# A Macaron block on one core: last attention pair two key blocks at a time, packed reciprocals, moved norm groups and half-width stores

## The chip, the cores and the metric

The kernel runs on one core of one Trainium2 chip. The metric is the device time of one execution in microseconds. Lower is better. The kernel before was run three times for this metric, and once more with the hardware profiler, whose page and trace are what the prediction is made from.

## The reference

The input x has 2048 tokens of 512 floats. The block is

```
x = x + 0.5 * ffn(layernorm(x))
x = x + attention(layernorm(x))
x = x + 0.5 * ffn(layernorm(x))
```

- `ffn` has a hidden size of 4096: `gelu(x @ Wg.T) * (x @ Wu.T)`, then `@ Wd.T`. The three weights come as 4-bit codes with one scale for every 32 values, and both calls use the same weights.
- `attention` is causal, with 16 heads of width 32: `softmax(q k.T / sqrt(32) + mask) v`, a projection in (with bias) and a projection out (with bias).
- `layernorm` subtracts the mean and divides by `sqrt(var + 1e-5)`, with no scale and shift.

All arithmetic is in f32.

## The kernel before

**Three stages.** FFN1 runs from 0 to about 1200 us, attention from about 1200 to 2135, FFN2 from 2135 to the end. x stays in on-chip memory throughout as 16 token tiles `xs` of 128 x 512. A matmul accumulates into a PSUM bank of 128 x 512 f32; the kernel has seven for short-lived results (`ps_one`) and one for the accumulator of attention (`ps_acc`). All instructions stand in the order in which Python emits them, and each engine works through its own queue in that order. DMAs are issued from SP's queue.

**FFN.** The hidden size is cut into 8 groups g of 512. `slot` (L292) computes gate and up for half a group and half the tokens by one level of Strassen: seven products in place of eight, for gate and again for up, so 14 pieces a slot. Sums of token blocks (`token_sums`, L261), of weights and of the results feed it. `down_pieces` (L358) does the product with Wd, also by seven pieces for each of two token pairs q, and adds the results into x. In FFN1 the weights are decoded on VectorE, and are kept in device memory for FFN2. The norms of token blocks 2 and 3 are not done before the FFN starts: `paced` (L138) splits them into groups, and the second slot of group 0 runs one group after each piece (L350). A norm is statistics on VectorE (L98), a square root on ScalarE (L107), a scaling on ScalarE (`xn`, L117) or VectorE, and four transposes on TensorE for each tile (`transpose`, L123). The same function places the norms for attention into the last pieces of FFN1 (L525 to L532). ScalarE also computes GELU (L307), so square root and GELU change its function table. `token_sums` of the second half runs on GpSimd in FFN1 and on VectorE in FFN2 (L482). In `down_pieces` additions that take two on-chip operands run on GpSimd (`add`, L396), and after the last piece of a q in the last group four tiles of x are stored (`finish`, L423).

**Attention.** Heads are taken in eight pairs p. The queries and keys of two pairs share a buffer of 128 partitions (`qT`, `kT`): pair p has rows 0 to 63 when p is even, 64 to 127 when it is odd, 32 rows to a head (`quadrant`, L623). A score matmul contracts over 32 rows, so it uses one quarter of the array's rows. The maxima of each query row must be known before its exponentials: `maxima(p)` (L635) computes scores once with queries on partitions, reduces them on VectorE (L669), splits the maximum into three bf16 parts (L678, GpSimd), and transposes them into `mrow` (L686). `attend(p)` (L699) then computes the scores again with keys on partitions. For a row block g of 512 queries and a block c of 128 keys it emits `maxrows` (a bf16 matmul of the three parts, L746) and `matmuls` (L755) into one bank for each head, and `rest`: on diagonal blocks a copy and a mask (L771, GpSimd's affine_select), then the exponentials on ScalarE (L778). `values` (L706) multiplies with v two blocks later (`pending`). The step loop (L870) runs `attend(p)` and `maxima(p + 1)` side by side, a block of each at a time, so that all four quadrants are in use; the last pair has nothing beside it.

**Denominators.** vaug has 32 columns of ones beside each head's values, so the accumulator holds each head's denominators in 32 identical rows. When row block g is done, ScalarE copies the accumulator into `both` (L720), two DMAs move the denominator rows to the partitions of the values (L725), and four chunks follow, one a step, from the third step on: a reciprocal of 128 x 128 on VectorE (L728) and two multiplies on GpSimd into `attnT` (L731). `divisions` (L736) is a list with one entry a step; it holds a division back on diagonal steps that also carry masks (L806).

**Fills.** Projections are put between diagonal steps: those of q, k and v for later pairs, and `project_out` (L611), whose pieces add `attnT @ wo` into x. In the last pair the pieces of o2 and o3 (of attnT 2 and 3) are spread over the four row blocks and, for g = 3, between steps (L858 to L861). The norms of token blocks 0 and 1 for FFN2 are placed there too (L862 to L868). The last four pieces (`o3[12:]`, L895) need the last chunks of pair 7.

Of the kernel before, what the change touches and what calls it, by code (L numbers as in the profile page):

```python
# [34 lines left out]
def macaron_kernel(ctx: ExitStack, tc: tile.TileContext, x, packed, scales, wqk, bqk, wv, bv, wo, bo, out):  # L35
# [26 lines left out]
    def load_x(tb):  # L62
# [12 lines left out]
    ones_b = const.tile([P, P], BF16, tag="ones_b", name="ones_b")  # L75
    nc.gpsimd.memset(ones_b, 1.0)
    identb = const.tile([P, P], BF16, tag="identb", name="identb")
    make_identity(nc, identb)

    mask_f = const.tile([P, P], F32, tag="mask_f", name="mask_f")  # L80
    nc.gpsimd.memset(mask_f, 0.0)
    nc.gpsimd.affine_select(
        out=mask_f, in_=mask_f, compare_op=ALU.is_ge, fill=MASKED, base=0, pattern=[[-1, P]], channel_multiplier=1
    )
    mask_b = const.tile([P, P], BF16, tag="mask_b", name="mask_b")
    nc.gpsimd.tensor_copy(mask_b, mask_f)
# [51 lines left out]
    def paced(first, second):  # L138

        a, b = [s[:2] + [s[2], s[3], s[5], s[7]] + [s[4], s[6], s[8], s[9]] for s in (first, second)]  # L140
        (a0, a1, *a), (b0, b1, *b) = a, b
        an, at, bn, bt = a[:4], a[4:], b[:4], b[4:]
        return [
            [a0], [a1], [b0, an[0]], [b1, an[1], at[0]], [an[2], at[1]], [an[3], at[2]],
            [bn[0], at[3]], [bn[1], bt[0]], [bn[2], bt[1]], [bn[3], bt[2]], [bt[3]],
        ]
# [7 lines left out]
    def ffn(phase, finish, behind, loads, ready=(), first_w=None):  # L154
# [8 lines left out]
        with tc.tile_pool(name=f"w{phase}", bufs=1) as wp, tc.tile_pool(name=f"dq{phase}", bufs=1) as dq, tc.tile_pool(  # L163
# [97 lines left out]
            def token_sums(tp, eng):  # L261
# [96 lines left out]
            def down_pieces(g, tp, wd, inter):  # L358
# [22 lines left out]
                def piece(i, q):  # L381
# [13 lines left out]

                    def add(dst, other):  # L396
                        nc.gpsimd.tensor_tensor(dst, dst, other, ALU.add)  # L397
# [7 lines left out]
                    elif i == 2:  # L405
                        from_bank(x11, x11)
                        add(x11, u[2, q])
                    elif i == 4:
# [7 lines left out]
                    elif i == 7:  # L416
                        from_bank(u[2, q], u[2, q])
                        add(x21, u[2, q])
                        add(x22, u[2, q])
                    else:  # L420
                        from_bank(u[4, q], u[4, q])
                        add(x12, u[4, q])
                        if g == NG - 1:  # L423
                            for t0 in (8 * tp + 2 * q, 8 * tp + 4 + 2 * q):
                                for t in (t0, t0 + 1):
                                    finish(t)
# [21 lines left out]
            def normed(nm):  # L448
                return ap.tile([P, D], F32, tag="u3", name=nm, bufs=2)
# [8 lines left out]
            if phase == 1:  # L458
# [14 lines left out]
                run(token_sums(0, nc.vector))  # L473
# [5 lines left out]
            else:  # L479
                run(token_sums(0, nc.vector))  # L480
            last_norms = paced(norms[2], norms[3])
            sums = token_sums(1, nc.gpsimd if phase == 1 else nc.vector)  # L482
            last_norms[-1].append(sums[0])
            last_norms += [[s] for s in sums[1:]]
# [49 lines left out]
    def attention(xT, xT_f, wqk_wv, next_w):  # L534
        with tc.tile_pool(name="aw", bufs=1) as aw, tc.tile_pool(name="qk", bufs=1) as qkp, tc.tile_pool(
# [7 lines left out]
            mrow = wo_bo[:, 5 * D :].bitcast(BF16)  # L543
            bqk_sb = aw.tile([P, 2, NQ], F32, tag="bqk", name="bqk_sb")
# [82 lines left out]
            later, divisions = [], []  # L627
# [7 lines left out]
            def maxima(p):  # L635
# [5 lines left out]
                for g in range(NB):  # L641
                    parts = an.tile([P, 2, 4, g + 1], F32, tag=f"parts{g}", name=f"parts_{p}_{g}")
                    steps = [(i, kb) for i in range(4) for kb in range(g)] + [(i, g) for i in (3, 2, 1, 0)]
                    for i, kb in steps:
# [28 lines left out]
                        def finish(now):  # L673
# [12 lines left out]
                            def rows(g=g, sp=sp):  # L686
                                h = slice(64 * (p % 2), 64 * (p % 2) + 64)
                                row = ps_one.tile([P, 512], BF16, tag="one", name=f"row_{p}_{g}")
                                for b in range(4):
                                    nc.tensor.transpose(row[h, bass.ts(b, P)], sp[:, b, :], identb)  # L690
# [8 lines left out]
            def attend(p):  # L699

                q, k, m = qT[(p // 2) % 2], kT[(p // 2) % 2], mrow
# [4 lines left out]
                def values(g, c, off, pt):  # L706
# [11 lines left out]
                    if c == 4 * g + 3:  # L718
                        both = an.tile([P, 512], F32, tag="both", name=f"both_{p}_{g}")
                        nc.scalar.copy(both, av)  # L720

                        rc = dens[g % 2]
                        for a in range(2):
                            v0, d0 = (0, HD) if a == 0 else (3 * HD, 2 * HD)
                            nc.sync.dma_start(out=rc[v0 : v0 + HD, :], in_=both[d0 : d0 + HD, :])  # L725

                        def chunk(j):
                            nc.vector.reciprocal(rc[:, bass.ts(j, P)], rc[:, bass.ts(j, P)])  # L728
# [7 lines left out]
                        divisions.extend([None] * 2 + [lambda j=j: chunk(j) for j in range(4)])  # L736

                for g in range(NB):
                    for c in range(4 * g + 4):
                        off = max(0, c - 4 * g) * P  # L740
                        ps = [None, None]

                        def maxrows(a):
                            r = quadrant(p, a)
                            ps[a] = ps_one.tile([P, 512], F32, tag="one", name=f"ps_{p}_{g}_{c}_{a}")
                            nc.tensor.matmul(  # L746
                                ps[a][:, off:],
                                lhsT=ones_b[r.start : r.start + 3, :],
                                rhs=m[r.start : r.start + 3, g * 512 + off : (g + 1) * 512],
                                start=True, stop=False,  # L750
                            )

                        def matmuls(a):
                            r = quadrant(p, a)
                            nc.tensor.matmul(  # L755
                                ps[a][:, off:],
                                lhsT=k[r, bass.ts(c, P)],
                                rhs=q[r, g * 512 + off : (g + 1) * 512],
                                start=False, stop=True,
                            )  # L760

                        def rest():
                            pt = pp.tile([P, 2, 512], F32, tag="pt", name=f"pt_{p}_{g}_{c}")
                            scale = 1.0 / math.sqrt(HD)
                            plain = off
                            if c >= 4 * g:

                                plain = off + P
                                own = pt[:, :, off:plain]
                                for a in range(2):  # L770
                                    nc.scalar.copy(own[:, a], ps[a][:, off:plain])  # L771
                                nc.gpsimd.affine_select(
                                    out=own, in_=own, compare_op=ALU.is_ge, fill=MASKED, base=0,
                                    pattern=[[0, 2], [1, P]], channel_multiplier=-1,
                                )
                            if plain < 512:
                                for a in range(2):
                                    nc.scalar.activation(pt[:, a, plain:], ps[a][:, plain:], AF.Exp, scale=scale)  # L778
                            if plain > off:
                                nc.scalar.activation(own, own, AF.Exp, scale=scale)  # L780
                            pending.append(lambda args=(g, c, off, pt): values(*args))
                            if len(pending) > 2:
                                pending.pop(0)()

                        yield maxrows, matmuls, rest, c >= 4 * g
# [14 lines left out]
            def after_step(diagonal, fill, masks):  # L800
# [4 lines left out]

# [182 lines left out]
```

## Time and profile before

| | us |
|---|---|
| median of three runs | 3313.41 |
| lowest, highest | 3310.98, 3314.13 |
| the profiled execution | 3312.17 |
| its span | 3310.4 |
| last pair of attention, with its tail | 2013.45 to 2135.38 |
| TensorE busy in the span | 3265.4 |
| VectorE busy | 2117.7 |
| GpSimd busy | 1153.2 |
| ScalarE busy | 870.3 |

The mean granted clock of TensorE was 0.998. The profiled execution lies 1.8 us above its span and 1.2 us below the median.

Reading it: PE is TensorE's matmul, PEld its weight load, DVE is VectorE, ACT ScalarE, POOL GpSimd, SP the engine that issues DMAs (SPq its queue). A line of the timeline gives the start, the duration, the engine, the line of the code, the operation with output and input, its shapes, and how many were joined into the line; brackets give the idle time before it and what ended it. In a table by windows each engine has its busy time and number of instructions, then come the granted clock (1.00 is full), the share of DMA time and GB/s.

### The profile page before, as it was taken

Reading aid. Unit: us, or ns where it says so; the run is one execution under the profiler, and the core shown is the slowest. Engines: PE = TensorE matmul, PEld = TensorE weight load, DVE = VectorE, ACT = ScalarE, POOL = GpSimd, SP = SyncE. Lnnn points to the kernel's source line nnn. Section 1 sums busy time; section 2 is a strip of 40 time slices with the busy share of each in tenths; the row PEclk is TensorE's granted clock in tenths of the full one; section 3 lists DMA queues with packets and bytes.
Section 4 is the critical chain, followed back from the end, with each engine's and each line's share of the span. In section 5 each row is a group of like instructions: output and inputs, shape, how many; then the busy total and the mean of one; then the engine's idle time right before and its main releaser. Section 6 shows DMA issues by size and latency. Waiting matters only on the chain.

```text
span 3310.4 us, 34022 instructions
## 1 busy us (share of the span) xinstructions
PE 3265.4 (99%) x12640; PEld 1724.7 (52%) x12640; DVE 2117.7 (64%) x3222; ACT 870.3 (26%) x1798; POOL 1153.2 (35%) x1333
## 2 busy tenths in 40 slices
PE   7999999999999999999999999999999999999998
PEld 3556565655656565333343333346555565655556
DVE  7977777777778556686766784455455455445545
ACT  4111111111111131454444555431111111111111
POOL 2646464554637341332221222103132222313223
PEclk9999999999999999999999999999999999999999
DMA  3111111111111100000000000100011101101101
GB/s 133 61 57 64 64 48 64 70 61 52 63 64 48 67 16 9 4 14 7 12 6 4 30 6 7 48 23 29 38 45 45 45 23 45 36 31 47 43 23 51
DMA packets 37943, 132.75 MB, mean 40 GB/s; under 512 B 3984, under 2 KB 20368, under 8 KB 31376
## 3 DMA queue, kind: packets, MB, share of 16 engines
q1 hardware_dynamic: 37776, 130.57, 10.7%
q8 instruction: 100, 1.64, 0.2%
q14 instruction: 67, 0.55, 0.1%
HBM read 78.12 MB, written 48.23 MB: 38 GB/s over the span
## 4 chain that ended last, share of the span: by engine, by line
PE 95%; DVE 1%; issue 1%; ACT 1%; POOL 1%; DMA 0%; POOLq 0%; SPq 0%; DVEq 0%; ACTq 0%
PE po L386 23%; PE pu L287 23%; PE pg L287 22%; PE av L711 8%; PE pm L654 6%; PE pqk L577 3%; PE ps L746 3%; PE ps L755 2%; PE pp L616 2%; PE pv L594 2%; PE pt_f L127 0%; DVE parts L669 0%; PE pt_a L127 0%; PE row L690 0%; DVE st_f L100 0%
## 5 line engine op out<-in xcount | busy, mean ns | idle before, releaser
L386 PE MATMUL po<-wd,inter 128*128 128x256 f32 x2048 | 482.5, 379 | 0.0
L287 PE MATMUL pg<-xT_f,w 128*128 128x512 f32 x1024 | 477.8, 594 | 0.0
L287 PE MATMUL pu<-xT_f,w 128*128 128x512 f32 x1024 | 476.0, 592 | 0.0
L386 PEld LDWEIGHTS po<-wd,inter 128*128 128x128 f32 x2048 | 388.9, 190 | 155.1 <-issue 104.8
L397 POOL TENSOR_TENSOR x<-x,d 128x512 f32<-128x512 f32 x256 | 340.0, 1340 | 346.1 <-DVE d L394 171.8
L341 POOL TENSOR_TENSOR u<-u,u 128x512 f32<-128x512 f32 x128 | 163.4, 1277 | 836.4 <-ACT u L338 832.1
L669 DVE TENSOR_REDUCE parts<-pm 128x1 f32<-128x512 f32 (+3 forms) x640 | 367.3, 604 | 92.9 <-PE pm L654 81.5
L386 PE MATMUL po<-wd,s 128*128 128x256 f32 x1536 | 362.2, 379 | 0.0
L287 PE MATMUL pg<-xsum,w 128*128 128x512 f32 x768 | 355.6, 592 | 3.2 <-POOL xsum L269 1.3
L287 PE MATMUL pu<-xsum,w 128*128 128x512 f32 x768 | 355.7, 592 | 0.0
L386 PEld LDWEIGHTS po<-wd,s 128*128 128x128 f32 x1536 | 291.6, 190 | 116.3 <-issue 79.6
L654 PE MATMUL pm<-kT,qT 32*128 32x512 f32 (+3 forms) x1280 | 337.7, 574 | 0.5 <-DVE parts L669 0.4
L778 ACT ACTIVATE pt<-ps 128x512 f32<-128x512 f32 (+3 forms) x576 | 271.8, 530 | 149.1 <-PE ps L755 148.1
L711 PE MATMUL av<-pt,vaug 128*64 128x512 f32 (+3 forms) x1280 | 304.1, 554 | 0.8 <-ACT both L720 0.6
L287 PEld LDWEIGHTS pg<-xT_f,w 128*128 128x128 f32 x1024 | 195.3, 191 | 193.4 <-issue 180.1
L287 PEld LDWEIGHTS pu<-xT_f,w 128*128 128x128 f32 x1024 | 194.2, 190 | 190.8 <-issue 181.3
L755 PE MATMUL ps<-qT,kT 32*128 32x512 f32 (+3 forms) x1280 | 292.8, 531 | 0.0
L287 PEld LDWEIGHTS pg<-xsum,w 128*128 128x128 f32 x768 | 145.5, 190 | 148.6 <-issue 136.6
L287 PEld LDWEIGHTS pu<-xsum,w 128*128 128x128 f32 x768 | 145.7, 190 | 143.4 <-issue 136.6
L394 DVE SCALAR_TENSOR_TENSOR x<-po,x 128x512 f32<-128x512 f32 x192 | 131.6, 686 | 115.8 <-ACT d L401 85.6
L731 POOL TENSOR_TENSOR attnT<-both,den 32x128 f32<-32x128 f32 x256 | 115.7, 452 | 242.1 <-DVE den L728 173.3
L394 DVE SCALAR_TENSOR_TENSOR d<-po,d 128x512 f32<-128x512 f32 x192 | 131.8, 686 | 86.2 <-PE po L386 84.2
(129 smaller groups left out, 3650.1 us busy)
## 6 DMA issues: line engine op xcount, KB each, us to landing
kept<-wd SPq DMA_DIRECT2D x8, 1792.0 KB
wd<-kept SPq DMA_DIRECT2D x8, 1792.0 KB
x<-in_x SPq DMA_DIRECT2D x16, 256.0 KB
pk<-in_gate_codes SPq DMA_DIRECT2D x16, 256.0 KB
sc<-in_gate_scales SPq DMA_DIRECT2D x32, 128.0 KB
pk<-in_up_codes SPq DMA_DIRECT2D x16, 256.0 KB
sc<-in_up_scales SPq DMA_DIRECT2D x32, 128.0 KB
pk<-in_down_codes SPq DMA_DIRECT2D x16, 256.0 KB
```

What stands on the lines that cost most here:

```text
L287: nc.tensor.matmul(ps, lhsT=a[:, j, :], rhs=b[:, j, :], start=(j == 0), stop=(j == 1))
L341: nc.gpsimd.tensor_tensor(u4, u4, u2, ALU.add)
L386: nc.tensor.matmul(ps[:, j, :], lhsT=a[i][:, k, bass.ts(2 * q + j, P)], rhs=b[i][:, k, :], start=(k == 0), stop=(k == 1),)
L394: stt(dst, ps, 0.5, other, ALU.mult, ALU.add)
L397: nc.gpsimd.tensor_tensor(dst, dst, other, ALU.add)
L577: nc.tensor.matmul(ps, lhsT=w[:, j, k, :], rhs=xT[tb][:, k, :], start=(k == 0), stop=(k == 3))
L654: nc.tensor.matmul(ps[a][:, :n], lhsT=q[r, bass.ts(4 * g + i, P)], rhs=k[r, kb * 512 : kb * 512 + n], start=True, stop=not on_pe,)
L669: nc.vector.tensor_reduce(parts[:, a, i, kb : kb + 1], ps[a][:, :n], AX.X, ALU.max)
L711: nc.tensor.matmul(av[64 * a : 64 * a + 64, off:], lhsT=vaug[:, c, p % 4, HD * a : HD * a + 2 * HD], rhs=pt[:, a, off:], start=(c == 0), s ...
L731: nc.gpsimd.tensor_tensor(dst[quadrant(p, a), bass.ts(4 * g + j, P)], both[v, bass.ts(j, P)], rc[v, bass.ts(j, P)], ALU.mult,)
L755: nc.tensor.matmul(ps[a][:, off:], lhsT=k[r, bass.ts(c, P)], rhs=q[r, g * 512 + off : (g + 1) * 512], start=False, stop=True,)
L778: nc.scalar.activation(pt[:, a, plain:], ps[a][:, plain:], AF.Exp, scale=scale)
```

## The change

1. **Last pair.** `attend` takes a width. Pair 7 is done with width 2: each step holds two key blocks, and their scores use all four quadrants. For this, at the start of pair 6, two DMAs copy rows 64 to 127 of pair 7's q and k to rows 0 to 63 of the other buffer, and the rows of maxima of pair 7 are transposed into both halves of `mrow`. Twice as many PSUM banks are taken by a step. The pieces of `project_out` that stood in the last diagonal steps stand after the loop, in front of and behind the last divisions.
2. **Reciprocals.** For pairs 0 to 6 one denominator row for each head goes by DMA to device memory (`flat`), comes back as 16 x 64 (`packs`), gets one small reciprocal four steps later, and goes back to device memory and, broadcast, to `den`. The multiplies follow from eight steps after the copy. Pair 7 keeps the direct way. `divisions` is keyed by step and holds nothing back.
3. **Norms and sums.** In `paced` the first normalised tile comes one group later, after both statistics groups of the second block; the list for the second slot starts with an empty group and takes the last three sums of `token_sums` in one group. `token_sums` is always on VectorE. xn has buffers of its own in place of those of u3.
4. **End.** In the last group, for the second half of tokens and q = 1, the additions run on VectorE. x is stored in quarters of a pair of tiles (two tiles, half the columns), each as soon as it is complete.
5. **Constants.** `ones_b`, `identb`, `mask_f` and `mask_b` are made at the start of attention.

```diff
@@ def paced
-            [a0], [a1], [b0, an[0]], [b1, an[1], at[0]], [an[2], at[1]], [an[3], at[2]],
+            [a0], [a1], [b0], [b1, an[0]], [an[1], at[0]], [an[2], at[1]], [an[3], at[2]],
             [bn[0], at[3]], [bn[1], bt[0]], [bn[2], bt[1]], [bn[3], bt[2]], [bt[3]],
@@ ffn
-            def token_sums(tp, eng):
+            def token_sums(tp):
+                eng = nc.vector
...
+                    adder = nc.vector if (g, tp, q) == (NG - 1, 1, 1) else nc.gpsimd
                     def add(dst, other):
-                        nc.gpsimd.tensor_tensor(dst, dst, other, ALU.add)
+                        adder.tensor_tensor(dst, dst, other, ALU.add)
+                    def done(second, half, x_):
+                        if g == NG - 1:
+                            finish(8 * tp + 2 * q + 4 * second, half, x_)
...
-                return ap.tile([P, D], F32, tag="u3", name=nm, bufs=2)
+                return ap.tile([P, D], F32, tag="xn", name=nm, bufs=2)
...
-            sums = token_sums(1, nc.gpsimd if phase == 1 else nc.vector)
+            sums = token_sums(1)
+            last_norms = [[]] + last_norms
             last_norms[-1].append(sums[0])
-            last_norms += [[s] for s in sums[1:]]
+            last_norms.append(sums[1:])
@@ maxima
-                                h = slice(64 * (p % 2), 64 * (p % 2) + 64)
+                                halves = (p % 2,) if p + 1 < NPAIR else (0, 1)
+                                h = slice(64 * halves[0], 64 * halves[-1] + 64)
...
-                                    nc.tensor.transpose(row[h, bass.ts(b, P)], sp[:, b, :], identb)
+                                    for i in halves:
+                                        nc.tensor.transpose(row[64 * i : 64 * i + 64, bass.ts(b, P)], sp[:, b, :], identb)
@@ values
+                        direct = p == NPAIR - 1
...
+                            flat = store.tile([2, 512], F32, tag=f"flat{g % 2}", name=f"flat_{p}_{g}")
+                            packs = an.tile([16, 64], F32, tag="packs", name=f"packs_{p}_{g}")
+                            for a in range(2):
+                                d0 = HD + HD * a
+                                nc.sync.dma_start(out=flat[a : a + 1, :], in_=both[d0 : d0 + 1, :])
+                            nc.sync.dma_start(out=packs, in_=flat.rearrange("a (j n) -> (a j) n", j=8))
+                        def inverse():
+                            nc.vector.reciprocal(packs, packs)
+                            back = store.tile([2, 512], F32, tag=f"back{g % 2}", name=f"back_{p}_{g}")
+                            nc.sync.dma_start(out=back.rearrange("a (j n) -> (a j) n", j=8), in_=packs)
+                            for a in range(2):
+                                v0 = 3 * HD * a
+                                nc.sync.dma_start(out=rc[v0 : v0 + HD, :], in_=back[a].partition_broadcast(HD))
                         def chunk(j):
-                            nc.vector.reciprocal(rc[:, bass.ts(j, P)], rc[:, bass.ts(j, P)])
+                            if direct:
+                                nc.vector.reciprocal(rc[:, bass.ts(j, P)], rc[:, bass.ts(j, P)])
...
-                        divisions.extend([None] * 2 + [lambda j=j: chunk(j) for j in range(4)])
+                        if not direct:
+                            at(4, inverse)
+                        for j in range(4):
+                            at((3 if direct else 8) + j, lambda j=j: chunk(j))
@@ attend
+                    i = 0 if copied else (p // 2) % 2
+                    q, k = qT[i], kT[i]
+                    def rows_of(a):
+                        return slice(HD * a, HD * a + HD) if copied else quadrant(p, a)
...
-                    for c in range(4 * g + 4):
+                    for c in range(0, 4 * g + 4, width):
+                        yield [step(g, c + i, i > 0) for i in range(width)]
@@ the loop over pairs
-                    fills = [o2[:4], o2[4:8], o2[8:12] + o3[:4], o2[12:] + o3[8:12]]
+                    fills = [o2[:4], o2[4:8], o2[8:12] + o3[:4], []]
...
+                if p + 2 == NPAIR:
+                    for t in (qT, kT):
+                        nc.sync.dma_start(out=t[0][0:64, :], in_=t[1][64:128, :])
+                n = 0
+                for steps in attend(p, 2 if p + 1 == NPAIR else 1):
...
                     for a in range(2):
-                        maxrows(a)
+                        for maxrows, _, _, _ in steps:
+                            maxrows(a)
...
                     for a in range(2):
-                        matmuls(a)
+                        for _, matmuls, _, _ in steps:
+                            matmuls(a)
...
-                    rest()
-                    after_step(diagonal, fill, other is not None)
-                    for step in extra.get(n, ()):
-                        step()
+                    for _, _, rest, _ in steps:
+                        rest()
+                    for _, _, _, diagonal in steps:
+                        after_step(diagonal, fill)
+                        for step in extra.get(n, ()):
+                            step()
+                        n += 1
...
-            for step in divisions:
-                if step:
+            rest = o2[12:] + o3[8:12]
+            for piece in rest[:4]:
+                piece()
+            for when in sorted(divisions):
+                for step in divisions[when]:
                     step()
-            for piece in o3[12:]:
+            for piece in rest[4:] + o3[12:]:
                 piece()
@@ the output
+    def store_out(t, half, x_):
+        rows = out[t * P : (t + 2) * P, half * 256 : half * 256 + 256]
+        nc.sync.dma_start(out=rows.rearrange("(j p) n -> p j n", p=P), in_=x_)
```

## The prediction, made before the changed kernel ran

> **What bounds the kernel now.** I read the page's first part, the chain that ended last, then the timeline by stage.
>
> ```profile
> PE 3265.4 (99%) x12640; PEld 1724.7 (52%) x12640; DVE 2117.7 (64%) x3222; ACT 870.3 (26%) x1798; POOL 1153.2 (35%) x1333
> ...
> PE 95%; DVE 1%; issue 1%; ACT 1%; POOL 1%; DMA 0%; POOLq 0%; SPq 0%; DVEq 0%; ACTq 0%
> ```
>
> TensorE is busy 99% of 3310.4 us and is 95% of the chain. Time taken from another engine counts only where TensorE waits for it, and such places sum to some 45 us. So two things can pay: fewer TensorE microseconds, or one of the few idle places.
>
> One block of scores in attention, first in pair 6 (which also computes the maxima of pair 7), then in pair 7 (which has no next pair):
>
> ```profile
> 1999.84 0.38 PE L746 MATMUL ps<-wo_bo,ones_b 3*128 3x512 bf16 x1
> 1999.84 0.69 PE L654 MATMUL pm<-kT,qT 32*128 32x512 f32 x1
> ...
> 2000.06 0.60 PE L755 MATMUL ps<-qT,kT 32*128 32x512 f32 x2
> 2000.37 0.60 PE L654 MATMUL pm<-kT,qT 32*128 32x512 f32 x2
> 2000.49 0.60 PE L755 MATMUL ps<-qT,kT 32*128 32x512 f32 x2
> 2001.02 1.08 PE L711 MATMUL av<-pt,vaug 128*64 128x512 f32 x4
> 2002.03 0.38 PE L746 MATMUL ps<-wo_bo,ones_b 3*128 3x512 bf16 x1
> ```
>
> ```profile
> 2050.80 0.39 PE L746 MATMUL ps<-wo_bo,ones_b 3*128 3x512 bf16 x2
> ...
> 2051.03 1.02 PE L755 MATMUL ps<-qT,kT 32*128 32x512 f32 x4
> ...
> 2051.98 1.08 PE L711 MATMUL av<-pt,vaug 128*64 128x512 f32 x4
> ...
> 2052.99 0.39 PE L746 MATMUL ps<-wo_bo,ones_b 3*128 3x512 bf16 x2
> ```
>
> The reader is to see one thing: 1999.84 to 2002.03 is 2.19 us, and 2050.80 to 2052.99 is 2.19 us as well. Four row quadrants (two of scores, two of maxima) take the 1.18 us that two take. Half the rows of the array stand empty in pair 7.
>
> The end of attention:
>
> ```profile
> 2122.92 0.87 PE L711 MATMUL av<-pt,vaug 128*64 128x256 f32 x8
> 2129.36 6.19 PE L616 MATMUL pp<-wo_bo,attnT 128*128 128x512 f32 x8 [5.56 <-POOL attnT L731]
> 2135.38 1.88 PE L287 MATMUL pg<-xT_f,w 128*128 128x512 f32 x4
> ```
>
> ```profile
> 2013.50:2123.80 110.30, 110.09 (x502) 37.17 (x500) 43.91 (x73) 58.31 (x140) 22.54 (x54) 1.00 0.02 6
> 2123.80:2129.40 5.60, 0.04 (x1) 0.05 (x1) 2.26 (x3) 0.59 (x1) 0.92 (x3) 0.84 0.10 23
> 2129.40:2135.40 6.00, 6.00 (x9) 2.52 (x10) 3.18 (x5) 0.00 (x0) 2.69 (x6) 0.58 0.00 0
> ```
>
> TensorE waits 5.56 us for copy, DMA, reciprocal and multiply, and then runs its last four pieces at a granted clock of 0.58: 6.19 us for what takes 4 x 1.06 = 4.24 elsewhere.
>
> **Last pair by two blocks.** By width 512, 384, 256, 128 the scores of a block took 1.18, 0.91, 0.66, 0.43 us. Before: 24 full blocks and four diagonals, 24 x 1.18 + 4 x 3.18 = 41.0 us. After, with both blocks of a step side by side and the wider one setting the time: 12 x 1.18 + 4 x (1.18 + 0.66) = 21.5. That takes away 19.5 us. The values (1.01 us per full block) stay.
>
> Eight projection pieces (8.5 us) leave the last diagonals and stand between the last values and the four dependent pieces. The last pair becomes 110.3 - 19.5 - 8.5 = 82.3 us, the tail 12 x 1.06 = 12.7 us. The first multiply ends about 5.5 us after the last values and the last one 8.7 us after, so 8.5 us of pieces cover the chain and the clock stays up. Together 95.0 against 121.9 (2013.45 to 2135.38): -26.9 us if nothing waits.
>
> Something will wait. The Trainium skill, "TensorEngine Tiling (Array Packing)", section Performance Considerations, speaks against this edit: packing speeds TensorE but not the emptying of PSUM, which may become the bottleneck. The rows: four exps are 2 x 1.08 = 2.16 us of ScalarE per double step, against 1.18 + 2 x 1.01 = 3.20 us on TensorE, so by the row the steady steps stay TensorE's and the whole 26.9 stand. But a double step holds four of the seven banks where a single one held two, so a ScalarE pause once covered by three steps is now covered by less than one. There is such a pause:
>
> ```profile
> 2083.22 1.28 ACT L107 ACT_TABLE_LOAD   x1
> 2086.47 0.30 ACT L107 ACTIVATE rstd_f<-mv_f,eps 128x4 f32<-128x4 f32 x1 [1.96 <-DVE mv_f L101]
> 2086.78 1.28 ACT L778 ACT_TABLE_LOAD   x1
> ```
>
> The square root of the norms stops the exps from 2083.22 to 2088.08, 4.86 us, without a TensorE wait today. In the new order its statistics stand on VectorE behind a reciprocal of the same row block that waits for its DMA, so I make the pause 6 us and the stall 6 less about 2 of cover: 4.0. The second norm group, placed the same way: 2.8. The first double step of three row blocks, where the copy of the accumulator stands behind four exps: 3 x 0.9. The last diagonals, without pieces between them (VectorE and GpSimd chain mask, exp, values): 1.65. The start: 0.3. Sum 11.5; bounds 0 and 18 (all of this plus a cold clock). By the row -26.9, by the rule's logic **-15.4**, which I take.
>
> Two copies of 512 KB (q and k rows 64 to 127 to rows 0 to 63) go onto SP's queue at the start of pair 6, ahead of the denominators of pair 5; a pair (over 80 us) lies before their first reader: 0, at worst 3 us once. The rows of maxima of pair 7 are transposed for both halves: four times four more transposes; a set took 0.39 us, so up to 1.6, and I take **+1.2**.
>
> **Packed reciprocals** (pairs 0 to 6, 28 places). Removed: 4 x 0.94 us of VectorE each (the reciprocal of den, 128 times, 119.6 us busy), less about 0.2 for the packed one: some 100 us of VectorE. TensorE's waits for VectorE or the accumulator copy in all pairs sum to 1 us, so this is worth about **0**. It adds a chain: copy 0.59, two issues of 0.51, landing 1.93, issue 0.51, landing 1.93, about 6 us, before a reciprocal emitted four steps later; four steps are 8.8 us in the long stretches, and about 5.8 at the shortest. Then back and two broadcasts (5 to 6 us) before multiplies four steps further on. Two of its hops go through device memory and no near row exists; bounds -3 (the three longest steps at the first row block of a pair lose some of their VectorE wait) and +22 (below). If it is late, behind the waiting reciprocal stand the maxima's reductions, with two banks each; behind the waiting multiply stand the mask operations.
>
> **Norm groups later, sums on VectorE.** In each FFN's second slot the second block's square root now comes before the first block's normalisation, so ScalarE's table changes square root, GELU, square root, GELU: two more loads per slot. Row: a load is 1.28 us and the next exp starts 1.30 after it. The skill, "ScalarE: Activation LUTs", What ACT_TABLE_LOAD costs, has 2.66 us per switch with the drain; the trace shows no such drain. By the row the first normalised tile of FFN1 comes at 65.0 instead of 59; by the page some 2.8 us later still, in both slots (forecast 5.6 us up). I take the row. FFN1's slot ran 35.4 us against 27.75 of work (waits 3.27, 0.64, 1.14, then 1.26 for GpSimd's xsum, and a clock of 0.66 after the longest). Later: one wait of 5.7 with the same cold stretch after it, and VectorE's sums (1.22 to 1.36 us against 2.35 to 2.80) remove the last wait: **-0.8**. FFN2's slot ran 33.1 (waits 1.01, 2.06, 1.14, clock 1.00); one wait of 4.85 and cold: **+1.4** (0.7 to 2.1). The norms at FFN1's end (waits 0.59 and 1.46 today): **+1.0** (0 to 2.5). Between FFN1 and attention the statistics come a little later: **+0.6**; the constants moved there (six GpSimd operations) run while GpSimd is free. xn's own buffers: 0 or a small gain.
>
> **The end.**
>
> ```profile
> 3301.16 3.71 POOL L397 TENSOR_TENSOR x<-x,d 128x512 f32<-128x512 f32 x3 [0.81 <-DVE d L394]
> ...
> 3304.90 2.00 SPq L923 DMA_DIRECT2D out<-x  x4
> ```
>
> Four stores follow the last sum, and the span ends at 3310.4. With the last additions on VectorE (0.69 where GpSimd takes 1.25) the last sum is done about 1.1 us sooner, and one store instead of four remains behind it (3 x 0.5): **-2.7** (-1.5 to -3.5).
>
> **Sum.** -15.4 + 1.2 + 0 - 0.8 + 1.4 + 1.0 + 0.6 - 2.7 = -14.7 us. The profiled execution took 3312.2 (span 3310.4 and 1.8 around it), giving 3297.5; the median of the runs is 3313.4, giving **3299**.
>
> **Rivals.**
> - *No stalls in the double steps.* For it: ScalarE is at 58.3 of 110.3 us in the last pair. Against: the 4.86 us pause and four banks a step. -14.7 - 11.5 = -26.2: 3287.
> - *The gain is given back in place.* Stalls of 18 instead of 11.5, and the page's table cost for 2 to 3 us: -14.7 + 6.5 + 2.5: 3308. For it: 0.58 after a wait of 5.56, 0.66 after 3.27. Against: 1.00 after 2.06.
> - *Slower: the packed chain is late.* The reciprocal waits on VectorE in order, the reductions behind it hold the banks of maxima, and TensorE stops at each of 28 places. One step of cover (2.2) is allowed for; it decides from (14.7 + 6.6) / 28 = 0.76 us each, that is from about 5.8 + 2.2 + 0.76 = 8.8 us between the last values and the landing. At 1.0 us each: 3299 + 28 = 3327. Against: my 6 us.
> - *Packing does not pay* when all four quadrants carry maxima rows and scores: only tail and end are left, about 3313 - 7: 3306. The 2.19 in both pairs speaks against it.
>
> **Chances.** Forecast 0.50, no stalls 0.22, given back or not paying 0.22, late chain 0.06. A measurement of this kernel tells about 0.2% (6.6 us) from no change. Faster 0.84 (all but half of the third case and the last), same 0.10, slower 0.06. The range 3285 to 3309 leaves out the late chain, the top of the third case and the bottom of the second.
>
> **What would show it.** Right: pair 7 with double steps of 3.2 us and a stall by the square root near its 15th; no 0.58 stretch before FFN2; four more table loads; one store after the last sum. Wrong: TensorE waiting in pairs 0 to 6 with VectorE's packed reciprocal as releaser, or double steps of 4.4 us.

## The result and the profile after

The changed kernel took 3298.16 us (median of five runs, 3296.2 to 3300.15) against 3312.97 for the kernel before, a ratio of 0.9956 with a 95% interval of 0.9941 to 0.9970: 14.8 us faster. The forecast was 3299. The profiled execution is the slowest of the five (3300.15, span 3298.4), so its span is 12.0 us shorter than that of before. One of the five executions of e1 below, the profiled one, ran at a granted clock of 0.65 and took 4810 us; it is left out, so no trace of e1 is read.

The parts of the page that answer to those shown of before, engines and chain:

```profile
PE 3249.1 (99%) x12656; PEld 1723.4 (52%) x12656; DVE 2043.7 (62%) x3152; ACT 872.9 (26%) x1802; POOL 1128.3 (34%) x1319
...
PE 94%; DVE 3%; ACT 2%; issue 1%; POOL 0%; DMA 0%; SPq 0%; POOLq 0%; DVEq 0%; ACTq 0%
```

TensorE has 16.3 us less work and is as full as before; VectorE has 74 us less, and what that is worth is tried in e2. Where the 12.0 us went is read by cutting both traces at the same instructions:

| stretch | before | after | difference |
|---|---|---|---|
| start to first gate product | 22.8 | 24.0 | +1.2 |
| to the first down product (holds FFN1's second slot) | 89.0 | 88.5 | -0.5 |
| to the first q/k projection (holds the norms at FFN1's end) | 1088.4 | 1090.5 | +2.1 |
| to the first scores of pair 0 | 100.7 | 100.7 | 0.0 |
| pairs 0 to 6 | 711.8 | 710.6 | -1.2 |
| pair 7 and tail, to FFN2's first product | 122.7 | 107.0 | -15.7 |
| to FFN2's first down product (holds its second slot) | 84.2 | 89.7 | +5.5 |
| to FFN2's last product | 1082.2 | 1082.2 | 0.0 |
| to the end of the span | 8.6 | 5.3 | -3.4 |

The start differs by 0.2 to 1.2 us among the executions of kernels that have the same code there; it is not the change. Pairs 0 to 6 took 711.8 us before, in e3 and in e9, and 713.4 in e4 and e10, whose code there is also that of before; with packed reciprocals they took 709.1 in e2, e6 and e7, and 710.4 to 710.8 in the changed kernel, e5, e8 and e11. In every case the longer ones have a stretch of 3.4 us at half clock between 1410 and 1420 us into the span, and the shorter ones do not. So the -1.2 of the table is -2.7 from the reciprocals and +1.5 from that stretch.

Pair 7 in the changed kernel, TensorE's timeline and then ScalarE's, around the first square root:

```profile
2075.00 0.39 PE L790 MATMUL ps<-wo_bo,ones_b 3*128 3x512 bf16 x4
2075.23 1.03 PE L799 MATMUL ps<-qT,kT 32*128 32x512 f32 x8
2076.18 1.94 PE L729 MATMUL av<-pt,vaug 128*64 128x512 f32 x8
...
2079.11 0.39 PE L790 MATMUL ps<-wo_bo,ones_b 3*128 3x512 bf16 x2
2082.12 0.86 PE L790 MATMUL ps<-wo_bo,ones_b 3*128 3x512 bf16 x2 [2.63 <-ACT pt L822]
2082.62 1.38 PE L799 MATMUL ps<-qT,kT 32*128 32x512 f32 x8
```

```profile
2074.36 1.28 ACT L95 ACT_TABLE_LOAD   x1
2079.87 0.30 ACT L95 ACTIVATE rstd_f<-mv_f,eps 128x4 f32<-128x4 f32 x1 [4.22 <-DVE mv_f L89]
2080.18 1.28 ACT L822 ACT_TABLE_LOAD   x1
2081.48 2.07 ACT L822 ACTIVATE pt<-ps 128x512 f32<-128x512 f32 x4
```

Two blocks of scores now take the 1.18 us from 2075.00 to 2076.18 that one took before. Then the exps stop from 2074.36 to 2081.48, 7.1 us, and TensorE, with half its maxima rows of the next step already out, finds no free bank for 2.63 us. That is what the prediction named; what its sum did not hold is in the last line of the first view, where 1.03 has become 1.38: soon after the wait TensorE runs at half clock, 0.50 in the third column from the end.

```profile
2083.58:2086.98 3.40, 3.40 (x12) 0.77 (x8) 0.00 (x0) 2.06 (x4) 0.17 (x1) 0.50 0.00 0
```

A table by windows, pair 7 and its tail (the column before the last two is the granted clock):

```profile
2014.27:2110.73 96.46, 87.43 (x495) 30.94 (x493) 35.66 (x64) 57.26 (x143) 22.69 (x54) 0.95 0.03 6
2110.73:2121.29 10.56, 10.56 (x26) 4.42 (x26) 8.97 (x14) 0.59 (x1) 3.61 (x8) 1.00 0.06 13
```

The clock was 1.00 in this stretch before. It is 0.95 now: three stretches of 3.4 us at half clock. The tail is full and at full clock.

The tail and FFN2's start, TensorE, then VectorE:

```profile
2110.66 10.79 PE L625 MATMUL pp<-wo_bo,attnT 128*128 128x512 f32 x24
2121.29 3.60 PE L276 MATMUL pg<-xT_f,w 128*128 128x512 f32 x8
...
2126.86 5.37 PE L276 MATMUL pg<-xsum,w 128*128 128x512 f32 x8 [1.98 <-issue]
```

```profile
2115.01 3.38 DVE L765 RECIPROCAL den<-den 128x128 f32<-128x128 f32 x4
...
2118.30 4.81 DVE L628 TENSOR_TENSOR x<-pp,x 128x512 f32<-128x512 f32 x8
...
2123.03 1.22 DVE L256 TENSOR_TENSOR xsum<-xT_f 128x1024 f32<-128x1024 f32 x1
```

Twelve pieces take 10.6 us, 0.88 each when they stand in a row. But their additions on VectorE are held up by the reciprocals, eight of them end at 2123.1, and only then come the sums of tokens that FFN2's third product needs. TensorE waits 1.98 us (1.05 before), and those products take 5.37 us for 3.6 at half clock.

The first norm tile of FFN1's second slot, and the end of the kernel (SP's queue and VectorE):

```profile
65.66 1.13 PE L115 MATMUL pt_f<-ident,xn_f 128*128 128x128 f32 x4 [4.95 <-ACT xn_f L105]
```

```profile
3293.24 2.30 SPq L985 DMA_DIRECT2D out<-x  x3
3293.73 0.68 DVE L383 SCALAR_TENSOR_TENSOR d<-po,d 128x512 f32<-128x512 f32 x1
3294.45 0.69 DVE L389 TENSOR_TENSOR x<-x,d 128x512 f32<-128x512 f32 x1
```

One wait has taken the place of three, as forecast. At the end one store, the third of the first line (issued at 3295.17), is left behind the last addition.

### The profile page after: what moved, and what is told of

The parts are those of the page before. It is cut to its first block, busy times and chain, and to the rows that moved or that the text cites. A ratio compares the mean times of both kernels' runs of the same rounds, so it can differ in the third digit from the quotient of the medians.

```text
span 3298.4 us, 34148 instructions
## 1 busy us (share of the span) xinstructions
PE 3249.1 (99%) x12656; PEld 1723.4 (52%) x12656; DVE 2043.7 (62%) x3152; ACT 872.9 (26%) x1802; POOL 1128.3 (34%) x1319
## 4 chain that ended last, share of the span: by engine, by line
PE 94%; DVE 3%; ACT 2%; issue 1%; POOL 0%; DMA 0%; SPq 0%; POOLq 0%; DVEq 0%; ACTq 0%
PE po L375 23%; PE pu L276 23%; PE pg L276 22%; PE av L729 8%; PE pm L668 6%; PE pqk L586 3%; PE ps L790 2%; PE pp L625 2%; PE pv L603 2%; PE ps L799 2%; ACT pt L822 1%; DVE st_f L88 0%; PE pt_f L115 0%; PE pt_a L115 0%; DVE parts L683 0%
## 5 line engine op out<-in xcount | busy, mean ns | idle before, releaser
L389 POOL TENSOR_TENSOR x<-x,d 128x512 f32<-128x512 f32 x248 | 329.7, 1340 | 344.7 <-DVE d L383 170.8
L799 PE MATMUL ps<-qT,kT 32*128 32x512 f32 (+3 forms) x1280 | 277.5, 534 | 0.0
L816 POOL TENSOR_SCALAR_AFFINE_SELECT pt<-pt 128x256 f32<-128x256 f32 x128 | 52.1, 407 | 388.0 <-ACT pt L815 387.8
```

The lines of the kernel that those rows point to most:

```text
L389: adder.tensor_tensor(dst, dst, other, ALU.add)
L799: nc.tensor.matmul(ps[a][:, off:], lhsT=k[r, bass.ts(c, P)], rhs=q[r, g * 512 + off : (g + 1) * 512], start=False, stop=True,)
```

## The experiments

All times are medians; ratios are to the kernel before on the same chip, with 95% intervals. The changed kernel, e1 to e4, e5 to e8 and e9 to e12 each ran beside a kernel before of their own, with medians of 3312.97, 3312.26, 3312.24 and 3312.35. So where a time of e5 to e12 is set against the changed kernel's 3298.16, 0.6 to 0.7 us of the gain is that difference. The intervals reach 2 to 4.5 us to either side; what small steps rest on is the stretches of the traces. My theory was the sum of the prediction: nearly all from the last pair, a little from the end, some lost on the norms. The rivals: the packed reciprocals carry part of the gain; the parts are only worth something together.

**Each part alone.** The kernel before with one part of the change. e1 has the last pair and its tail:

```diff
-                for n, (...) in enumerate(attend(p)):
+                for steps in attend(p, 2 if p + 1 == NPAIR else 1):
...
+            rest = o2[12:] + o3[8:12]
```

> Kernel before with the last-pair part alone (double steps, rows of maxima for both halves, pieces moved behind the loop). My theory, as in the prediction: -15.4 + 1.2 = -14.2 us. From the profile of the changed kernel: from the end of pair 6 to the first FFN2 product it took 107.0 us against 122.7, so -15.7. Rival, the packed reciprocals carry part of the gain: less than 12 us here.

Measured 3295.01, ratio 0.9945 (0.9932 to 0.9959): -17.3 us. The rival (under 12 us) falls. The gain is more than the theory's 14.2, and more than the whole change brought.

e2 has the packed reciprocals (`flat`, `packs`, `inverse`, chunks from the eighth step):

> Kernel before with the packed reciprocals alone (pairs 0 to 6). My theory: 0 us, within 1. Rival, the chain costs: slower by 5 or more. Second rival, VectorE's 100 us do count: faster by 3 or more. In the profile of the changed kernel pairs 0 to 6 are 1.2 us shorter.

Measured 3309.03, ratio 0.9991 (0.9983 to 0.9999): -3.2 us, at the edge of what can be told from nothing and more than my 0. The trace says where. The starts of all 280 steps of pairs 0 to 6 were compared: one step in each of row blocks 1, 2 and 3, the third, where the accumulator of the row block before is copied, went from about 3.0 to 2.8 us, together -3.7 over the seven pairs; a few others gave back 1.0, which leaves the -2.7 of pairs 0 to 6 in this trace. One such step of pair 3 before:

```profile
1663.82 0.94 DVE L728 RECIPROCAL den<-den 128x128 f32<-128x128 f32 x1
...
1664.49 0.59 PE L654 MATMUL pm<-kT,qT 32*128 32x512 f32 x1
...
1664.68 1.22 DVE L669 TENSOR_REDUCE parts<-pm 128x1 f32<-128x512 f32 x2
...
1666.03 0.38 PE L746 MATMUL ps<-wo_bo,ones_b 3*128 3x512 bf16 x1
```

and with packed reciprocals:

```profile
1663.27 1.41 DVE L683 TENSOR_REDUCE parts<-pm 128x1 f32<-128x512 f32 x2 [0.50 <-PE pm L668]
1663.36 0.59 PE L668 MATMUL pm<-kT,qT 32*128 32x512 f32 x1
...
1664.91 0.39 PE L790 MATMUL ps<-wo_bo,ones_b 3*128 3x512 bf16 x1
```

Before, a reciprocal of 0.94 us stands on VectorE between two pairs of reductions. After, VectorE is waiting for TensorE there. The step before ran from 1663.02 to 1666.03, now from 1662.11 to 1664.91. That the reductions gave the banks back late is read from these lines; it was not tried by itself.

e3 has the norm groups, the sums and xn's buffers (with the moved constants, whose room they take):

```diff
-            [a0], [a1], [b0, an[0]], [b1, an[1], at[0]], ...
+            [a0], [a1], [b0], [b1, an[0]], [an[1], at[0]], ...
```

> Kernel before with the moved norm groups, token sums on VectorE, xn's own buffers and the moved constants (these two belong together, since the buffers take the room of the constants). My theory as in the prediction: -0.8 + 1.4 + 1.0 + 0.6 = +2.2 us. From the profile of the changed kernel: -0.5 in FFN1's slot, +2.1 at FFN1's end and up to +5.4 in FFN2, so about +7. Rival, the part gains because the three short waits become one: -3.

Measured 3316.42, ratio 1.0012 (1.0006 to 1.0019): +4.2 us. The part costs time, more than the prediction's +2.2 and less than the +7 read from the changed kernel. Its trace has the wait of 4.29 us in each slot, -0.5 for FFN1's slot, +0.5 at FFN1's end and +2.4 in FFN2's. The -0.5 is not the part's doing: in e2, e4, e9 and e10, whose code there is that of before, the same slot is 0.5 to 0.8 us shorter than in the one trace of before.

e4 has the end (`adder`, `done`, `store_out`):

> Kernel before with the end alone (last additions on VectorE, output stored by halves). My theory: -2.7 us. From the profile of the changed kernel: -3.4. Rival, the smaller stores cost more at the queue: 0 or slower.

Measured 3309.48, ratio 0.9990 (0.9982 to 0.9998): -2.8 us; in its trace the stretch after the last product is 3.5 us shorter.

The four sum to -17.3 - 3.2 + 4.2 - 2.8 = -19.1, against -14.8 for all. The four intervals together are about as wide as that difference, so it is not shown that the parts work against each other. The granted clock is where the difference could lie: it was 0.997 to 0.998 in the four runs of e1 and 0.994 or 0.995 in the five of the changed kernel, and 0.001 of 3300 us is at most 3.3 us of TensorE's time (an estimate; half clock under a wait costs less).

**The last pair in two halves.** e9 has the double steps, with the pieces where they were; e10 only moves the pieces, by this edit:

```diff
-                    fills = [..., o2[12:] + o3[8:12]]
+                    fills = [..., []]
```

> Kernel before with the double steps alone: the pieces of the output projection stay in the last diagonal steps. My theory: scores -19.5 us, stalls and half clock in the last pair +7, transposes +1.2, the tail as before: about -11. Rival, the double steps bring nearly all of the -17.3 that both together measured: -15 or more.

Measured 3300.98, ratio 0.9967 (0.9954 to 0.9979): -11.4 us, as the theory had it; the rival falls. Pair 6, in which 12 of the 16 added transposes stand, took 81.49 us in its trace and in that of before.

> Kernel before with the moved pieces alone: the last pair stays at one block a step. My theory: the wait of 5.56 us and the half clock of about 1.9 go, -7.4, less about 1 where the last diagonal steps lose their cover: -6. Rival, the half clock only moves to FFN2's start (its wait for the sums of tokens): -4.

Measured 3305.24, ratio 0.9979 (0.9973 to 0.9986): -7.1 us. The trace adds what the total hides: the last pair and tail are 8.0 us shorter and FFN2's beginning 2.9 us longer, by the wait already seen in the changed kernel, here with one block a step:

```profile
2128.34 3.60 PE L287 MATMUL pg<-xT_f,w 128*128 128x512 f32 x8
2133.92 5.37 PE L287 MATMUL pg<-xsum,w 128*128 128x512 f32 x8 [1.98 <-issue]
```

So the moved pieces alone make it. The rival had the right place, the theory the better size. In the traces e9 and e10 shorten pair 7 and tail by 11.5 and 8.0 us, and the changed kernel, with both, by 15.7; by the medians they sum to -18.5, against -17.3 in e1. Whether the two gains overlap stays open.

**The norms.** e5 takes the norm part out of the changed kernel (the constants stay moved):

> Changed kernel with the norm groups, the token sums and the xn buffers as before. My theory now: the norm part costs what it cost alone, +4.2, and some 3 us more that only the whole change shows in FFN2, so 3298.2 - 4 to 7 = 3291 to 3294. Rival, the parts are not additive because of the last pair alone: about 3298, no change.

Measured 3293.21, ratio 0.9942 (0.9930 to 0.9955): 4.9 us under the changed kernel (4.2 when each is taken against its own kernel before), which agrees with e3.

e6 swaps two steps in one group, so that the first tile is normalised before the second half of the second block's statistics and its square root:

```diff
-            [a0], [a1], [b0], [b1, an[0]], [an[1], at[0]], ...
+            [a0], [a1], [b0], [an[0], b1], [an[1], at[0]], ...
```

> Changed kernel with two steps of one norm group swapped: the first normalised tile is emitted before the second half of the second block's statistics, so before its square root. My theory, the wait of about 5 us in each second slot comes from this tile standing behind the second square root and the two table loads before it: the wait of 4.95 in FFN1 and 4.29 in FFN2 falls under 3, and the time by 4 to 8 us. Rival, VectorE's statistics are what is late whatever the order on ScalarE: within 1 us of the changed kernel.

Measured 3290.89, ratio 0.9935 (0.9922 to 0.9947): 7.3 us under the changed kernel (6.5 against its own kernel before). FFN1's slot is 2.4 us shorter than the changed kernel's, FFN1's end 3.9, FFN2's slot 1.9. The wait of 4.95 in FFN1's slot became

```profile
62.52 0.74 PE L115 MATMUL pt_f<-ident,xn_f 128*128 128x128 f32 x4 [2.67 <-ACT xn_f L105]
...
66.77 0.74 PE L115 MATMUL pt_f<-ident,xn_f 128*128 128x128 f32 x4 [1.79 <-ACT xn_f L105]
```

4.46 us of waiting in two pieces, and in this execution no half clock at all in FFN1, where the changed kernel had 6.8 us of it in the slot and 3.4 at the end. The swap changes nothing in the order of VectorE's queue, so the order on ScalarE is the cause, and not VectorE's statistics. About half of the gain is the clock: of the 8.2 us in these three stretches 4.0 are waits of TensorE and 4.2 its busy time.

e7 fills the wait with matmuls whose result is not used:

```diff
+            def warm():
+                ps = ps_one.tile([P, 512], F32, tag="one", name=f"warm_{phase}")
+                for _ in range(4):
+                    product(ps, second.factors(0)[1], token_factors(0)[1])
```

> Changed kernel with 8 matmuls of 128x512 more (3.4 us at full clock, result unused) on TensorE in each second slot, just before the first transpose that waits. If the half clock after the wait is a cost of its own (6.8 us at half clock in each slot, so 3.4 us lost), these slots are 2 to 3.4 us shorter each, the time 4 to 7 us. Rival, the clock costs nothing beyond the wait or goes down anyway: 0, or longer by what does not fit into the wait.

Measured 3299.31, ratio 0.9959 (0.9947 to 0.9972): no change, where the theory had 4 to 7 us. The eight matmuls took 7.03 us and not the 3.4 I had put down:

```profile
60.08 7.03 PE L276 MATMUL warm<-xT_f,w 128*128 128x512 f32 x16
```

That still answers the question: 7.03 us of work put in the place of a 4.95 us wait made FFN1's slot 0.25 us shorter. Wait and half clock together had cost 7.03 + 0.25 = 7.3 us, so the half clock about 2.3 of them. That is for this one place. For the changed kernel and then this one, the windows of the wait and of the work after it, and of the filled stretch:

```profile
60.60:65.60 5.00, 0.11 (x1) 0.00 (x0) 4.13 (x12) 3.52 (x5) 0.65 (x1) 0.73 0.11 46
65.60:72.50 6.90, 6.80 (x18) 3.45 (x19) 1.01 (x2) 4.74 (x8) 0.00 (x0) 0.70 0.00 0
```

```profile
50.00:66.00 16.00, 16.00 (x38) 7.03 (x37) 13.27 (x31) 9.08 (x12) 5.03 (x5) 1.00 0.32 132
66.00:84.50 18.50, 18.46 (x67) 10.17 (x66) 6.71 (x10) 11.44 (x19) 1.27 (x1) 1.00 0.00 0
```

**The square roots.** e8 does those of pair 7 on VectorE: an integer shift and subtraction for a first value, and three Newton steps, 12 instructions on 128 x 4 (the expectation counts 13):

```diff
-                nc.scalar.activation(rstd, mv[:, :, 1], AF.Sqrt, bias=eps)
-                nc.vector.reciprocal(rstd, rstd)
+                if not on_act:
+                    inverse_root()
+                else:
+                    ...
```

> Changed kernel with the two square roots of the last attention pair done on VectorE (13 small instructions, by shift, subtraction and three Newton steps) instead of ScalarE, so without the four table loads there. My theory, the pause of ScalarE stops the double steps: the wait of 2.63 us and the half clock after it go, 3 to 5 us faster than the changed kernel. Rival, the pause is covered and the stall has to do with VectorE's order: 0.

Measured 3294.71, ratio 0.9942 (0.9929 to 0.9956): 3.5 us under the changed kernel (2.7 against its own kernel before), at the low end of the theory. In its trace pair 7 and tail are 3.6 us shorter. The wait of 2.63 for a bank is gone, so the pause of ScalarE was its cause; one of 1.25 for VectorE's normalised tile stands there, and 2.75 at the second block. All idle time of TensorE in pair 7 is 8.7 us for 9.0, so most of the gain is in its busy time, with two stretches of half clock there in place of three.

e11 is both, the version to which the experiments point:

> Changed kernel with the swapped norm steps of e6 and the square roots of the last pair on VectorE of e8. If both causes are separate, the gains add: 3298.2 - 7.3 - 3.5 = 3287, against 3312.3 before. Rival, both only bring the clock back once: about 3290.

Measured 3286.88, ratio 0.9924 (0.9912 to 0.9937): 25.5 us faster than before, 11.3 than the changed kernel. That is the sum of the two gains. The rival's 3290 lies within the interval, so the traces decide: against the changed kernel, FFN1's slot is 2.4 us shorter, FFN1's end 3.8 and FFN2's slot 1.9, as in e6, and pair 7 and tail 5.9, for 3.6 in e8. The two causes are separate.

Its pair 7 shows once more what the clock is worth, since its code there is that of e8. The last pair up to its last values in e8, then in e11:

```profile
2012.40:2105.28 92.88, 84.15 (x497) 30.20 (x493) 39.18 (x87) 51.80 (x137) 22.66 (x54) 0.96 0.03 7
```

```profile
2006.92:2097.50 90.58, 81.23 (x497) 29.56 (x493) 39.20 (x87) 51.57 (x137) 22.67 (x54) 1.00 0.03 7
```

The same work is 84.2 us busy at 0.96 and 81.2 at 1.00. Half clock need not cost time, though: FFN1's slot has 3.4 us of it in e11 and none in e6, with the same code, and took 86.1 us in both. In e11 it follows the first wait (2.68), and the second wait (1.79 in e6) is gone.

e12 takes all the other square roots but those of the first two blocks to VectorE as well:

> As e11, with the square roots of the norms in both second slots, at FFN1's end and at attention's start on VectorE too, so that ScalarE's table changes no more for them. If the table loads hold the first normalised tile, its waits in the slots (2.67 in e6) fall under 1.5 and the time is 2 to 4 us under e11. Rival, the 13 small instructions on VectorE take as long as the loads they replace: within 1 us of e11.

Measured 3302.92, ratio 0.9973 (0.9962 to 0.9983): 16 us over e11. Both theories fall. The instructions are not what they were in pair 7. At FFN1's end, VectorE, then GpSimd:

```profile
1179.26 1.12 DVE L97 TENSOR_SCALAR rstd_a<-root_t_a 128x4 int32<-128x4 int32 x1
1180.41 1.18 DVE L99 TENSOR_TENSOR root_t_a<-rstd_a 128x4 f32<-128x4 f32 x1
1181.63 0.16 DVE L100 SCALAR_TENSOR_TENSOR root_t_a<-root_t_a,mv_a 128x4 f32<-128x4 f32 x1
...
1191.48 0.17 DVE L97 TENSOR_SCALAR rstd_a<-root_t_a 128x4 int32<-128x4 int32 x1
```

```profile
1179.07 1.28 POOL L378 TENSOR_TENSOR s<-inter,s 128x512 f32<-128x512 f32 x1
1180.32 1.26 POOL L375 TENSOR_TENSOR s<-inter,inter 128x512 f32<-128x512 f32 x1
```

The same instruction takes 1.12 us while GpSimd runs one addition after another, and 0.17 later, when GpSimd has stopped. The slow ones end with GpSimd's instruction: 1180.38 beside 1180.35, then 1181.59 beside 1181.58. The Trainium skill, "SBUF — State Buffer", section "SBUF: two separate sides", states a rule that fits: VectorE and GpSimd share a pair of ports as an exclusive lock, and a VectorE instruction that needs the pair (one with two inputs in on-chip memory, or in a mode that takes both ports) waits for the whole of a GpSimd instruction that came first. This chain of twelve small steps ran from 1178.47 to 1187.04, 8.6 us; the next one, beside an idle GpSimd, took 2.3.

That is one chain of ten; none of the others took over 3.4 us. In the traces e12 is longer than e11 by 8.6 us at FFN1's end, where this chain stands, by 5.4 in FFN1's slot, 3.4 in FFN2's, 2.4 in pair 7 and tail, whose code is the same, and 1.8 ahead of the first scores. In FFN1's slot a chain of 3.3 us stands in VectorE's queue ahead of the slot's own pieces, and the GELU in front of the first normalised tile on ScalarE waits for one of these:

```profile
66.08 0.63 ACT L311 ACTIVATE c<-c 128x512 f32<-128x512 f32 x1 [5.16 <-DVE c L344]
66.61 0.80 ACT L120 ACTIVATE xn_f<-x,nbias_f,rstd_f 128x512 f32<-128x512 f32 x1
```

So for the slot the longer queue is read from the trace as the cause, and for FFN1's end the lock; neither was tried by itself.

## Why the prediction was right, and where it was not

The total was right to 1 us. Some terms were not, and they cancelled. That it came so close is luck: runs of the changed kernel alone spread by 4 us.

- **Double steps.** Right: two blocks in 1.18 us. Full sum for pair 7 without stalls, from its first step to its last values: 111.1 - 19.5 - 8.5 = 83.1; measured 96.46, so 13.4 lost where the prediction had 11.5 of stalls. Its 1.2 for transposes did not show (pair 6 took 81.49 us with and without them). The make-up was different: waits of 8.7 us in all (stats 2.63 where I had 4.0; second norm group 1.6 for 2.8; the copies of the accumulator 1.3 for 2.7; diagonals and start 3.2 for 1.95), and about 4.7 of half clock and rest, which the sum had at nothing and only the bound held. "A cold clock" should have been a term: three stretches of 3.4 us at half speed are at most 5.1 us lost.
- **The rule on PSUM.** The rows alone gave -26.9 for pair and tail, the rule's logic -15.4. Measured -15.7. The rule was the better guide, by way of the banks and not of ScalarE's total: ScalarE was 57 of 96 us busy. That -15.7 lies so near -15.4 is chance, for the 1.9 us more that the pair lost stand against 2.1 less in the tail.
- **Tail.** 12.7 was mis-sized: 10.6, since pieces in a row take 0.88 and not the 1.06 that they take between steps. Worth 2.1 us. "The clock stays up" was right for the tail.
- **FFN2's slot.** +1.4 was the step that failed: +5.5. Its waits are 7.2 us for 5.3, and TensorE's busy time 82.4 for 78.9, which is the half clock. Two causes, both tried: the norm part (+2.4 in e3), and one that the prediction did not have at all, the eight additions which the moved pieces put on VectorE ahead of FFN2's token sums (+2.9 in e10). Of a moved step I had costed TensorE's matmuls and not its VectorE instruction.
- **Other norm terms.** FFN1's slot -0.8, measured -0.5, which code unchanged there shows too (e2, e4, e9, e10), so about 0. FFN1's end and the boundary +1.6 (1.0 and 0.6), measured +2.1 and 0.0 here and +0.5 and 0.0 in e3 with the same code: a wait of 2.79 in both, followed by half clock in one only. The whole part: forecast +2.2, alone +4.2.
- **The rule on table loads.** By the row the first tile of FFN1's slot comes at 65.0, by the page 2.8 us later; its transpose started at 65.66, with the whole execution 1.2 us late. The row was right.
- **Packed reciprocals.** 0, bounds -3 and +22; measured -3.2. "TensorE's waits for VectorE sum to 1 us" was the wrong test: the gain was in steps that were longer before (3.0 for 2.8) with no idle time of TensorE in them. That TensorE waits for a bank there is read from the lines of e2, not tried.
- **End.** -2.7, alone -2.8.
- **Rivals.** The late chain did not come: in the changed kernel none of the 28 packed reciprocals (0.53 us each) had a wait before it. e11 reaches the 3287 of "no stalls" without being that case: TensorE is idle for 9.3 us of its pair 7, and part of its gain comes from the norms.

What is open: whether the parts bring less together than singly, for the runs do not separate 14.8 from 19.1.

## What to carry to other kernels

When a step is moved to fill one engine's gap, write down every instruction that goes with it, and look at what stands behind each of them in its own queue: here the filled tail of attention made FFN2 wait. A wait on TensorE can cost more than its length, because half clock may follow (7.3 us for a wait of 4.95 in FFN1's slot), so give it a term of its own; here it ranged from nothing to some 2 us. And before an engine change is written, look at the order in a queue: one swap of two steps was worth 7.3 us, about half of what the whole change brought.

## What the hardware showed that I had not expected

- Half clock came in stretches of 3.4 us or twice that, and followed waits that were short: 1.46 us in pair 7 of the changed kernel (clock down from 2039.2) and 2.63, but not the 2.06 of FFN2's slot before. The Trainium skill, "TensorE: Matmul & The Clock Gate", Part 1, puts it at an idle stretch of one window, about 3.4 us, which these waits do not reach. Its section "A second HAM failure mode: psum-queue depth-cycling" puts it at many short gaps in another kernel. That does not settle it either: the three waits of FFN2's slot before (1.01, 2.06 and 1.14 within 9 us) brought none. What decides it is open.
- Identical code was hit in one execution and not in another, so that after the same 2.79 us wait FFN1's end took 0 or 1.7 us more. Runs of one kernel spread by 4 us.
- A VectorE instruction on 128 x 4 took 0.17 us beside an idle GpSimd, and up to 1.2 beside a busy one.
